# The rank-9 part of twelve chunks of a graph layer, read as nine more rows of the gathered lists

## The chip, the cores and the metric

The kernel runs on one core of one Trainium2 chip. The metric is the device time of one execution in microseconds (us); the number given is the median of several runs. The profile is one execution taken by the hardware profiler. Its engines are PE (TensorE matmuls), PEld (TensorE weight loads, which overlap PE), DVE (VectorE), ACT (ScalarE), POOL (GpSimdE) and SP (SyncE, which issues transfers). L361 means line 361 of the kernel.

## The reference, cut to what matters

There are B = 8 batches, N = 2048 nodes and D = 128 features. The matrix `adj` is 2048 x 2048, sparse: some nine entries in a row are not zero, the diagonal among them. Layer 0 and its normalisation:

```python
sj = inputs @ w_j
si = inputs @ w_i
res = si[:, :, None] + sj[:, None, :] + relation[None] * w_r + g_b
agg = jnp.einsum('bij,bjd->bid', res, inputs)
x = layernorm(x + agg @ weight + bias)
```

`res` is a sparse matrix (the relation) plus a sum of outer products. So `agg @ weight + bias` is a sparse product with y0 = x @ (weight * w_r), plus a part of low rank: node i of batch b gets si[b, i] times the sum over j of x[b, j] @ weight, plus one row that is the same for all nodes (the sj, g_b and bias terms). That is the rank-9 part: nine numbers per node (si of the eight batches, and a one) times nine rows of B x D = 1024 numbers.

Layer 1 makes two hops with `adj` itself, x1 = adj^T x and x2 = 2 adj^T x1 - x, times slices of Theta1, then bias, relu, residual and layernorm. It has no rank-9 part.

## The kernel before, in words

The nodes are cut into NC = 16 chunks of 128. A result chunk is a [128 nodes, 8 batches x 128 features] tile in two PSUM banks (`accs`).

*Opening.* Loops over the chunks load rows of `adj`, transpose them, store relation columns to DRAM (`store_rt`), make y0 (`y_chunk`, kept in `Y`) and the column sums of x, and mark which rows have entries in which block of 32 columns. `copy_r` copies `adj` columns beside the stored ones: `rr_d[c]` has, for each row n, 128 relation weights for layer 0 and 128 for layer 1. `si` holds for each chunk the eight numbers per node and a one; `make_ub` makes `ub`, the nine rows of 1024.

*Chunks 0 to 3 (ND = 4) of layer 0* are done densely (L720, all 16 row chunks). During that, the marks are turned into lists of row numbers. Each column chunk has seven: four quarter lists (rows needed by one block of 32 columns, at most eight from each row chunk, placed at that row chunk's eight places), two half lists (64 columns) and one for the whole chunk. A list has 128 places; its row numbers lie in a column of `idx`. An empty place holds PAD = 40000, past the bound of the gather, so that nothing is moved for it, and `has` is 0 there. The rows of a chunk itself are in no list: they are done as a dense diagonal block (`own_rows`, L781). `split` sets which ranks a list takes, and `lists_end` turns the found numbers into `idx` and `has`.

*Chunks 4 to 15 of layer 0* (in the order `seq`: 9 to 14, 4 to 8, 15) use the lists. For each list a gather takes rows of `rr_d` into a stage; `keep_r` (L620, L626) multiplies them by `has` and writes the columns wanted, for layer 0 into `rct` and for layer 1 into `rc`. `listed_rows` gathers the rows of y0 (from `y0_d`) into a ring of nine buffers, seven for a chunk, and multiplies them by those weights (L799): quarters, then halves, then the whole list. One round of the loop, for chunk c with the next chunk c1:

```python
            put(c)
            while jobs[0][0] == c1:
                gathers(1)
            sit = si_t(c)
            accs = acc_pair()
            own_rows(0, c, accs, True)
            rank1(c, accs, sit)
            listed_rows(0, y0_d, c, accs)
            make_u(*pending)
            z = finish0(c, accs, xr)
```

`si_t` transposes `si` on TensorE and has ScalarE copy it (L349), `rank1` does the rank-9 matmuls (L361), `make_u` takes the chunk before through transposes and a product with Theta to the store of `u`, and `finish0` adds x and normalises on VectorE and ScalarE.

*Order.* A scheduler orders each engine's instructions. `keep_in_program_order` pins an instruction behind all that was traced before it on its engine, so `keep_r(c)` comes after the layernorm of the chunk before. All gathers are chained in program order on GpSimdE, and the matmuls of `own_rows` and `listed_rows` among themselves on TensorE. The tiles of `rows4` (loads of x, `cs4`, `u`, transposed x) share five slots.

*Layer 1* makes its two hops over the same lists, from `u_d` and `y_d`, with the weights `rc`. A conditional block at the end, for matrices whose lists overflow, isn't taken here.

Of the kernel before, what the change touches and what calls it, by code (L numbers as in the profile page):

```python
# [8 lines left out]
F32 = mybir.dt.float32  # L9
# [9 lines left out]
def kernel(  # L19
# [44 lines left out]

    seq = list(range(NG4, NC - 1)) + list(range(ND, NG4)) + [NC - 1]
    PAD = 40000
    assert D == P and B == 8 and NT == 64

    y0_d = nc.dram_tensor("y0_d", (N, BD), F32).ap()
    rr_d = [  # L70
        nc.dram_tensor(f"rr_d{c}", (N, 2, P), F32).ap() for c in range(ND, NC)
    ]
    u_d = nc.dram_tensor("u_d", (N, BD), F32).ap()
    y_d = nc.dram_tensor("y_d", (N, BD), F32).ap()
# [201 lines left out]
    def store_rt():  # L276
        for c, at in stores:
            tc.keep_in_program_order(nc.sync.dma_start(
                out=rr_d[c - ND][:, 0, :].rearrange("(j p) i -> p j i", p=P), in_=at
            ))  # L280
        stores.clear()

# [62 lines left out]
    def si_t(c):  # L345
        pst = p_tr.tile([B + 1, P], F32, name=f"pst{c}", tag="pt")
        nc.tensor.transpose(pst, si[:, c, :], ident)
        sit = small.tile([B + 1, P], F32, name=f"sit{c}", tag="sit")
        nc.scalar.copy(sit, pst)  # L349
        return sit  # L350
# [7 lines left out]
    def rank1(c, accs, sit):  # L358

        for h in range(2):  # L360
            nc.tensor.matmul(  # L361
                accs[h], sit, ub[:, h * HB:(h + 1) * HB, :],
                start=False, stop=(c < ND), skip_group_check=True,
            )

    def finish0(c, accs, xr, norm=True):
# [26 lines left out]
    def copy_r(n0, n1):  # L393
        for c in seq[n0:n1]:
            tc.keep_in_program_order(
                nc.sync.dma_start(out=rr_d[c - ND][:, 1, :], in_=adj[:, c * P:(c + 1) * P])
            )

    copy_r(0, 2)


    wk = rc2[:, ND * CW:NC * CW]
    hit, two, alone = [
# [77 lines left out]
                start=False, stop=(c == NC - 2), skip_group_check=True,  # L481
            ))

    def split(rank, m, mn, lo, hi):

        nc.vector.tensor_mul(mn, m, rows_by(num, m.shape[2]))
        nc.vector.scalar_tensor_tensor(hi, rank, float(P), mn, op0=ALU.is_le, op1=ALU.mult)
        nc.vector.scalar_tensor_tensor(lo, rank, 64.0, mn, op0=ALU.is_le, op1=ALU.mult)

    def half_ranks():  # L490
        rank = p_tr.tile([P, NC, NH], F32, name="rank_h", tag="pt")
        ranks(rank, half)
        lo, hi = enc[:, :, 0:NH], enc[:, :, NH:2 * NH]
        split(rank, half, halfn, lo, hi)

        nc.vector.scalar_tensor_tensor(half, hi, 0.0, half, op0=ALU.is_equal, op1=ALU.mult)
        nc.vector.tensor_sub(hi, hi, lo)
        for t in range(2):
            nc.vector.tensor_add(both, both, pairs(half)[:, :, :, t])
# [3 lines left out]
    def chunk_ranks():  # L503
        rank = p_tr.tile([P, NC, NC], F32, name="rank_c", tag="pt")
        ranks(rank, both)
        lo, hi = enc[:, :, 2 * NH:2 * NH + NC], enc[:, :, 2 * NH + NC:96]
        split(rank, both, halfn.rearrange("p c w -> p (c w)")[:, 0:NC * NC].rearrange(
            "p (c w) -> p c w", w=NC), lo, hi)
        nc.vector.tensor_sub(hi, hi, lo)
        nc.vector.tensor_reduce(miss, both.rearrange("p c w -> p w c"), AX.X, ALU.add)  # L510

# [20 lines left out]
    def make_ub():  # L532
# [11 lines left out]
        for h in range(2):  # L544
# [3 lines left out]
                nc.tensor.matmul(pu[:, i, :], e8, b0row, start=False, stop=True)  # L548
            nc.vector.tensor_copy(ub[:, h * HB:(h + 1) * HB, :], pu)

    def lists_end(a, b, parts):

        pl = p_tr.tile([P, P], F32, name=f"pl{a}", tag="pt")
        for h, c0, src, p0, n in parts:
            tc.keep_in_program_order(nc.tensor.matmul(
                pl[64 * h:64 * h + 64, c0:c0 + n], src, ident[0:src.shape[0], p0:p0 + n],
                start=True, stop=True, skip_group_check=True, tile_position=(0, 64 * h),
            ))
        pli = pl[:, a:b]
        rown, row2 = [  # L560
            rct2[:, 5 * BD - n * P + a:5 * BD - n * P + b] for n in range(1, 3)
        ]

        nc.vector.tensor_scalar(rown, pli, 0.0, float(PAD + 1), op0=ALU.is_equal, op1=ALU.mult)
        nc.vector.scalar_tensor_tensor(rown, pli, -1.0, rown, op0=ALU.add, op1=ALU.add)
        nc.vector.tensor_copy(idx[:, a:b], rown)
        nc.vector.tensor_scalar(has[:, a:b], pli, 0.0, None, op0=ALU.is_gt)
        nc.vector.scalar_tensor_tensor(
            row2, rown, float(NC), col[:, a:b], op0=ALU.mult, op1=ALU.add
        )  # L570
        return nc.vector.tensor_copy(idr[:, a:b], row2)
# [32 lines left out]
    def gather_r(c, q, m, st, n):  # L604


        gather(
            st[:, n * m * P:(n + 1) * m * P],
            rr_d[c - ND].rearrange("n m f -> n (m f)") if m == 2 else adj128,
            idx if m == 2 else idr,  # L610
            4 * c + n if q else (LP + 2 * c, LP + 2 * c + 1, LF + c)[n], N if m == 2 else N * NC,
        )

    def keep_r(c, q, m, st):
# [54 lines left out]
    for c in range(ND):  # L669
        if c + 1 < ND:  # L670
            if NA <= c + 2 < ND:
                ar2 = load_rows(c + 2, wide[3])
            xr1 = load_x(c + 1, "xr", nc.sync)
        if c < 2:
            copy_r(2 + 5 * c, 7 + 5 * c)
        if 1 <= c <= 2:
            for n in range(8 * c - 8, 8 * c):
                tc.keep_in_program_order(
                    nc.sync.dma_start(out=y0_d[n * P:(n + 1) * P, :], in_=flat(Y[n]))
                )  # L680
        if c == 0:
            make_ub()
            rank1(0, accs, si_t(0))
        else:
            z = finish0(c, accs, xr, c > 2)
        if c + 1 < ND:
            accs1, sit = acc_pair(), si_t(c + 1)
            at2 = first_at.get(c + 2)
            for j in range(NC):
                if c == 0:  # L690
                    if j == 4:
                        tile_ranks()
                    if j == 7:
                        tile_lists()
                    if j == 10:
                        at = tile_lists_end()
                        half_ranks()
                    if j == 14:
                        chunk_ranks()
                        z = finish0(c, accs, xr, False)  # L700
                        layernorm(z, "0_0", at)
                if c == 1 and j < 2:
                    candidates(2 * j)
                    candidates(2 * j + 1)
                if c == 1 and (j > 1 and j % 2 == 0 or j == NC - 1):
                    list_round(j // 2 - (j < NC - 1))
                if c == 2:
                    if j == 4:
                        at = chunk_lists_end()
                        layernorm(z1, "0_1", at)  # L710
                    if j == 8:
                        layernorm(z, "0_2", at)
                if c > 0 or j > 11:
                    gathers(1 if j % 3 else 2, mm)
                if ar2 is not None and j % 2 == 0 and j >= 8:
                    if j == 8:
                        at2 = by_chunk(wide[0])
                    transpose_group(c + 2, ar2, at2, j // 2 - 4)
                for h in range(2):
                    mm = nc.tensor.matmul(  # L720
                        accs1[h], at1[:, j, :], Y[j][:, h * HB:(h + 1) * HB, :],
                        start=(j == 0), stop=False, skip_group_check=True,
                    )
            rank1(c + 1, accs1, sit)
            if c > 0:
                gathers(2, mm)
            at1, ar2, accs = at2, None, accs1
        if pending is not None:
            make_u(*pending)
        z1 = z  # L730
        pending, xr = (c, z, rows4(f"xt{c}")), xr1
# [54 lines left out]
    def listed_rows(i, src, c, accs):  # L786
        def rows_of(n):
            g = G[turn[2] % NG4]
            turn[2] += 1
            gather(g, src, idx, n, N)  # L790
            return g

        r = rc[:, c] if i else rct[:, c - ND]
# [12 lines left out]
    with nc.allow_non_contiguous_dma(reason="512-byte rows of a diagonal block"):  # L806
        fetch_own(0, y0_d, seq[0])
        xr = load_x(seq[0], "xs", nc.sync)
        for c, c1 in zip(seq, seq[1:] + [None]):
            if c1 is not None:  # L810
                fetch_own(0, y0_d, c1)
                xr1 = load_x(c1, "xs", nc.sync)
            put(c)
            while jobs[0][0] == c1:
                gathers(1)
            sit = si_t(c)
            accs = acc_pair()
            own_rows(0, c, accs, True)
            rank1(c, accs, sit)
            listed_rows(0, y0_d, c, accs)  # L820
            make_u(*pending)
            z = finish0(c, accs, xr)
            pending, xr = (c, z, x1t[c], held.get((1, c))), xr1
# [149 lines left out]
```

## Time and profile before

| | |
|---|---|
| time | 941.91 us, median of 3 runs (937.77 to 952.31) |
| span of the profiled execution | 945.7 us |
| busy: PE, PEld | 810.8 us (86%), 392.9 us (42%) |
| busy: DVE, ACT, POOL | 403.2 us (43%), 176.6 us (19%), 441.5 us (47%) |
| opening | 0 to 154 us |
| dense chunks and making of the lists | 154 to about 272 us |
| listed chunks of layer 0 | about 303 to 515 us |
| two hops of layer 1 | about 515 to 740 and 740 to 946 us |
| moved by transfers | 262.83 MB, 278 GB/s on the average |

The busy shares are averages over stages with different limits; what a change in one stage is worth is read from that stage. A group of the profile gives line, engine, operation, written and read tile, count, busy time and mean length, and then the idle time of the engine just before those instructions with what ended it. The chain of waits follows the work that ended last back to the start.

### The profile page before, as it was taken

How to read it: one execution, taken by the hardware profiler on the slowest of the kernel's cores; microseconds unless marked ns; L12 is line 12 of the kernel's file. 1: busy time of each engine (PE TensorE's matmuls, PEld its weight loads, DVE VectorE, ACT ScalarE, POOL GpSimd, SP SyncE). 2: the span in 40 equal slices, each digit the busy share in tenths (PEclk: the TensorE clock that was granted, in tenths of full speed). 3: DMA queues.
4: the chain of work that ended last, by engine and by line, in shares of the span. 5: the costliest groups of instructions: out<-in, count | busy, mean ns of one | idle time of the engine just before them, and what ended most of it. 6: DMA issues, size and time to landing. Idle time of an engine off the chain costs nothing.

```text
span 945.7 us, 10375 instructions
## 1 busy us (share of the span) xinstructions
PE 810.8 (86%) x3666; PEld 392.9 (42%) x3666; DVE 403.2 (43%) x627; ACT 176.6 (19%) x408; POOL 441.5 (47%) x431
## 2 busy tenths in 40 slices
PE   6999989999975878878889767889899898999992
PEld 4666653564432333423345222333333434444541
DVE  4465671539932444544345000000010045776676
ACT  3566650110111121121112000000000001111111
POOL 0000000046673676764540566767666356677750
PEclk9999998999995898987789899899999989999997
DMA  8699999962837888987775678989999689999992
GB/s 283 219 297 292 281 287 277 316 237 74 326 102 289 268 262 287 301 273 246 245 254 208 232 262 284 317 281 324 319 379 385 230 299 350 367 351 339 328 357 87
DMA packets 171183, 262.83 MB, mean 278 GB/s; under 512 B 17480, under 2 KB 122348, under 8 KB 168946
## 3 DMA queue, kind: packets, MB, share of 16 engines
q0 software_dynamic: 49280, 146.52, 44.8%
q1 hardware_dynamic: 98512, 87.83, 29.3%
q10 hardware_dynamic: 23330, 27.73, 8.3%
q8 instruction: 31, 0.51, 0.2%
q14 instruction: 30, 0.25, 0.1%
HBM read 241.63 MB, written 60.82 MB: 320 GB/s over the span
## 4 chain that ended last, share of the span: by engine, by line
PE 61%; DMA 14%; issue 11%; DVE 6%; ACT 4%; POOL 2%; another core or an unknown queue 1%; POOLq 0%; SPq 0%; ACTq 0%; DVEq 0%
PE acc L799 25%; PE acc L720 6%; DMA Y<-u_d,idx 6%; PE acc L781 5%; DMA Y<-y_d,idx 5%; PE acc L361 4%; PE acc L840 3%; PE acc L328 3%; PE acc L318 3%; PE pp L387 2%; POOL Y L592 2%; DVE rc L523 2%; PE pt_a L181 1%; ACT sq L212 1%; DMA rc<-in_adj_dram 1%
## 5 line engine op out<-in xcount | busy, mean ns | idle before, releaser
L799 PE MATMUL acc<-Y,rc 128*32 128x512 f32 (+2 forms) x896 | 245.5, 630 | 42.9 <-issue 19.1
L592 POOL DMA_INDIRECT Y<-y_d,idx x196 | 206.4, 1053 | 151.3 <-PE acc L799 91.7
L592 POOL DMA_INDIRECT stage<-rr_d,idx x84 | 94.2, 1121 | 230.4 <-PE acc L720 208.2
L592 POOL DMA_INDIRECT Y<-u_d,idx x112 | 111.3, 994 | 87.8 <-PE acc L781 30.8
L799 PEld LDWEIGHTS acc<-Y,rc 128*32 128x32 f32 (+2 forms) x896 | 63.1, 131 | 213.9 <-issue 142.3
L799 PE MATMUL acc<-Y,rct 128*32 128x512 f32 (+2 forms) x336 | 90.7, 861 | 0.0
L720 PE MATMUL acc<-Y,wide 128*128 128x512 f32 x192 | 88.2, 609 | 0.0
L361 PE MATMUL acc<-ub,sit 9*128 9x512 f32 x64 | 43.3, 807 | 36.5 <-ACT sit L349 25.8
L213 DVE TENSOR_REDUCE st<-sq 128x4 f32<-128x512 f32 x64 | 43.9, 686 | 60.5 <-ACT sq L212 31.0
L781 PE MATMUL acc<-Y,rd 128*128 128x512 f32 x140 | 67.7, 593 | 0.0
L173 DVE COPY z<-acc 128x512 f32<-128x512 f32 x9 | 6.2, 692 | 138.6 <-issue 50.4
L720 PEld LDWEIGHTS acc<-Y,wide 128*128 128x128 f32 x192 | 36.2, 195 | 41.6 <-issue 41.6
L799 PEld LDWEIGHTS acc<-Y,rct 128*32 128x32 f32 (+2 forms) x336 | 22.2, 163 | 73.3 <-issue 71.8
L212 ACT ACTIVATE sq<-z 128x512 f32<-128x512 f32 x32 | 20.1, 630 | 161.0 <-DVE z L208 105.4
L370 DVE TENSOR_TENSOR xs<-acc,xs 128x512 f32<-128x512 f32 x24 | 16.6, 692 | 78.1 <-PE acc L799 47.1
L181 PE MATMUL pt_a<-ident,rc 128*128 128x128 f32 x240 | 35.9, 286 | 7.3 <-DMA rc<-in_adj_dram 5.9
L289 DVE TENSOR_REDUCE rc<-rc 128x64 f32<-128x2048 f32 x16 | 36.5, 2282 | 13.0 <-DMA rc<-in_adj_dram 12.9
L318 PE MATMUL acc<-wx,tr_x 128*128 128x130 f32 x256 | 36.5, 286 | 3.9 <-ACT tr_x L175 3.1
L318 PEld LDWEIGHTS acc<-wx,tr_x 128*128 128x128 f32 x256 | 33.0, 195 | 14.4 <-ACT tr_x L175 6.4
L328 PE MATMUL acc<-Y,wide 128*128 128x512 f32 x64 | 36.7, 655 | 2.5 <-ACT Y L322 1.4
L361 PEld LDWEIGHTS acc<-ub,sit 9*128 9x128 f32 x64 | 13.0, 226 | 59.1 <-ACT sit L349 32.4
L181 PEld LDWEIGHTS pt_a<-ident,rc 128*128 128x128 f32 x240 | 29.4, 147 | 16.8 <-issue 14.5
(190 smaller groups left out, 935.6 us busy)
## 6 DMA issues: line engine op xcount, KB each, us to landing
rc<-in_adj_dram SPq DMA_DIRECT2D x16, 1024.0 KB
rr_d<-rct SPq DMA_DIRECT2D x12, 1024.0 KB
rr_d<-in_adj_dram SPq DMA_DIRECT2D x12, 1024.0 KB
xs<-in_x_dram SPq DMA_DIRECT2D x20, 512.0 KB
y_d<-Y SPq DMA_DIRECT2D x16, 512.0 KB
out_dram<-z ACTq DMA_DIRECT2D x16, 512.0 KB
u_d<-u ACTq DMA_DIRECT2D x14, 512.0 KB
Y<-y_d SPq DMA_DIRECT2D x14, 512.0 KB
```

What stands on the lines that cost most here:

```text
L181: nc.tensor.transpose(pt[:, i, :], s, ident)
L212: nc.scalar.activation(sq, z[:, hs, :], AF.Square)
L213: nc.vector.tensor_reduce(st[:, 2, hs], sq, AX.X, ALU.add)
L289: nc.vector.tensor_reduce(mk[:, c, :], a.rearrange("p (w f) -> p w f", f=TW), AX.X, ALU.max, apply_absolute_value=True,)
L318: nc.tensor.matmul(py[:, i, 0:D + 2], xt[b // HB][:, (b + i) % HB, :], wx, start=True, stop=True,)
L328: nc.tensor.matmul(acc0[h], first_at[0][:, c, :], Y[c][:, h * HB:(h + 1) * HB, :], start=(c == 0), stop=False, skip_group_check=True,)
L361: nc.tensor.matmul(accs[h], sit, ub[:, h * HB:(h + 1) * HB, :], start=False, stop=(c < ND), skip_group_check=True,)
L592: g = nc.gpsimd.indirect_dma_start(out=out, out_offset=None, in_=src, in_offset=bass.IndirectOffsetOnAxis(ap=ids[:, n:n + 1], axis=0), bou ...
L720: mm = nc.tensor.matmul(accs1[h], at1[:, j, :], Y[j][:, h * HB:(h + 1) * HB, :], start=(j == 0), stop=False, skip_group_check=True,)
L781: in_order(nc.tensor.matmul(accs[h], r, t[:, h * HB:(h + 1) * HB, :], start=start, stop=False, skip_group_check=True,))
L799: in_order(nc.tensor.matmul(accs[h][w * t:w * t + w], r[:, o + w * t:o + w * t + w], gs[t][:, h * HB * D:(h + 1) * HB * D], start=False, s ...
L840: in_order(nc.tensor.matmul(accs[h][:, b, :], x1t[c][:, h * HB + b, :], th[:, i, :], start=(b == 0), stop=False, skip_group_check=True,))
```

## The change

The nine numbers per node become nine more rows of weights, and the nine rows of `ub` nine more rows of y0: `y0_d` and each `rr_d[c]` get NX = N + 9 = 2057 rows. The lists then name these rows in places that no list fills. In the four quarter lists of a chunk, the eight places of its own rows are always empty: they name the eight rows of the batches. In the two half lists the last place is kept free (`most` is 127 there): it names the ninth row. The table `extra` holds what must be added to PAD in those places, and `lists_end` adds it. `more_rows`, called once before the dense chunk 0, stores the rows. Their layer 1 half is zero, and in the hops the bound of the gather stays N, so the nine rows aren't moved. The listed matmuls then do the rank-9 part of chunks 4 to 15; chunks 0 to 3 keep `rank1`. In short, with the unchanged parts left out:

```diff
-    y0_d = nc.dram_tensor("y0_d", (N, BD), F32).ap()
+    y0_d = nc.dram_tensor("y0_d", (NX, BD), F32).ap()
     rr_d = [
-        nc.dram_tensor(f"rr_d{c}", (N, 2, P), F32).ap() for c in range(ND, NC)
+        nc.dram_tensor(f"rr_d{c}", (NX, 2, P), F32).ap() for c in range(ND, NC)
...
+    extra = rct2[:, 5 * BD - 4 * P:5 * BD - 4 * P + NI]
+    nc.vector.memset(extra, 0.0)
+    xq = extra[:, 4 * ND:LP]
+    nc.vector.tensor_scalar(
+        xq, col[:, 4 * ND:LP], -8.0, num[:, 0:1], op0=ALU.mult, op1=ALU.add
+    )
...
+    nc.vector.tensor_scalar(far, extra, 0.0, None, op0=ALU.is_gt)
+    nc.vector.tensor_scalar(extra, extra, float(N - 1 - PAD), None, op0=ALU.add)
+    nc.vector.tensor_mul(extra, extra, far)
...
-        split(rank, half, halfn, lo, hi)
+        split(rank, half, halfn, lo, hi, P - 1)
...
+    def more_rows():
+
+        tc.keep_in_program_order(nc.sync.dma_start(out=y0_d[N:, :], in_=flat(ub)))
+        n = (NC - ND) * (B + 1)
+        ps = p_tr.tile([P, P], F32, name="ps", tag="pt")
+        nc.tensor.transpose(ps[0:n, :], si[:, ND:, :].rearrange("p c b -> p (c b)"), ident)
+        t = rows4("sit_all")
+        nc.vector.memset(t[:, 1, :], 0.0)
+        nc.scalar.copy(t[0:n, 0, :], ps[0:n, :])
+        for c in seq:
+            tc.keep_in_program_order(nc.sync.dma_start(
+                out=rr_d[c - ND][N:, :, :],
+                in_=t[(B + 1) * (c - ND):(B + 1) * (c - ND + 1), 0:2, :],
+            ))
...
+        nc.vector.tensor_add(rown, rown, extra[:, a:b])
         nc.vector.tensor_copy(idx[:, a:b], rown)
-        nc.vector.tensor_scalar(has[:, a:b], pli, 0.0, None, op0=ALU.is_gt)
+        nc.vector.tensor_scalar(has[:, a:b], rown, float(NX), None, op0=ALU.is_lt)
...
             make_ub()
+            more_rows()
             rank1(0, accs, si_t(0))
...
-            gather(g, src, idx, n, N)
+            gather(g, src, idx, n, src.shape[0])
...
-            sit = si_t(c)
             accs = acc_pair()
             own_rows(0, c, accs, True)
-            rank1(c, accs, sit)
             listed_rows(0, y0_d, c, accs)
```

More of the change, by code (lines that the diff above doesn't have):

```diff
@@ L66 @@
     PAD = 40000
+    NX = N + B + 1
     assert D == P and B == 8 and NT == 64
-    y0_d = nc.dram_tensor("y0_d", (N, BD), F32).ap()
+    y0_d = nc.dram_tensor("y0_d", (NX, BD), F32).ap()
     rr_d = [
-        nc.dram_tensor(f"rr_d{c}", (N, 2, P), F32).ap() for c in range(ND, NC)
+        nc.dram_tensor(f"rr_d{c}", (NX, 2, P), F32).ap() for c in range(ND, NC)
     ]
@@ L278, in store_rt @@
             tc.keep_in_program_order(nc.sync.dma_start(
-                out=rr_d[c - ND][:, 0, :].rearrange("(j p) i -> p j i", p=P), in_=at
+                out=rr_d[c - ND][0:N, 0, :].rearrange("(j p) i -> p j i", p=P), in_=at
             ))
@@ L362, in rank1 @@
                 accs[h], sit, ub[:, h * HB:(h + 1) * HB, :],
-                start=False, stop=(c < ND), skip_group_check=True,
+                start=False, stop=True, skip_group_check=True,
             )
@@ L395, in copy_r @@
             tc.keep_in_program_order(
-                nc.sync.dma_start(out=rr_d[c - ND][:, 1, :], in_=adj[:, c * P:(c + 1) * P])
+                nc.sync.dma_start(out=rr_d[c - ND][0:N, 1, :], in_=adj[:, c * P:(c + 1) * P])
             )
     copy_r(0, 2)
+    extra = rct2[:, 5 * BD - 4 * P:5 * BD - 4 * P + NI]
[4 more added lines that the diff above has]
+    )
+    far = rct2[:, 5 * BD - 3 * P:5 * BD - 3 * P + NI]
+    nc.vector.tensor_scalar(far[:, 4 * ND:LP], xq, float(B), None, op0=ALU.is_le)
+    nc.vector.tensor_mul(xq, xq, far[:, 4 * ND:LP])
+    nc.vector.tensor_scalar(far[:, 0:1], num[:, 0:1], float(P), None, op0=ALU.is_equal)
+    nc.vector.tensor_scalar(
+        extra[:, LP + 2 * ND:LF], far[:, 0:1].to_broadcast([P, NH - 2 * ND]), float(B + 1), None,
+        op0=ALU.mult,
+    )
+    nc.vector.tensor_scalar(far, extra, 0.0, None, op0=ALU.is_gt)
+    nc.vector.tensor_scalar(extra, extra, float(N - 1 - PAD), None, op0=ALU.add)
+    nc.vector.tensor_mul(extra, extra, far)
     wk = rc2[:, ND * CW:NC * CW]
@@ L482, in ranks, with split @@
             ))
-    def split(rank, m, mn, lo, hi):
+    def split(rank, m, mn, lo, hi, most):
         nc.vector.tensor_mul(mn, m, rows_by(num, m.shape[2]))
-        nc.vector.scalar_tensor_tensor(hi, rank, float(P), mn, op0=ALU.is_le, op1=ALU.mult)
+        nc.vector.scalar_tensor_tensor(hi, rank, float(most), mn, op0=ALU.is_le, op1=ALU.mult)
         nc.vector.scalar_tensor_tensor(lo, rank, 64.0, mn, op0=ALU.is_le, op1=ALU.mult)
@@ L507, in chunk_ranks @@
         split(rank, both, halfn.rearrange("p c w -> p (c w)")[:, 0:NC * NC].rearrange(
-            "p (c w) -> p c w", w=NC), lo, hi)
+            "p (c w) -> p c w", w=NC), lo, hi, P)
         nc.vector.tensor_sub(hi, hi, lo)
@@ L610, in gather_r @@
             idx if m == 2 else idr,
-            4 * c + n if q else (LP + 2 * c, LP + 2 * c + 1, LF + c)[n], N if m == 2 else N * NC,
+            4 * c + n if q else (LP + 2 * c, LP + 2 * c + 1, LF + c)[n], NX if m == 2 else N * NC,
         )
```

## The prediction

> **What bounds the kernel now.** I read the page's shares first, then its groups, then the busy time by stretch, then the chain of waits and the timeline of one chunk.
>
> ```profile
> PE 61%; DMA 14%; issue 11%; DVE 6%; ACT 4%; POOL 2%; another core or an unknown queue 1%; POOLq 0%; SPq 0%; ACTq 0%; DVEq 0%
> L361 PE MATMUL acc<-ub,sit 9*128 9x512 f32 x64 | 43.3, 807 | 36.5 <-ACT sit L349 25.8 <-issue 10.7
> L799 PE MATMUL acc<-Y,rct 128*32 128x512 f32 (+2 forms) x336 | 90.7, 861 | 0.0
> ```
>
> TensorE carries 61% of the chain. The rank-9 matmuls (L361) stand out twice: 43.3 us busy, and 36.5 us of idle TensorE just ahead of them, 25.8 of it put down to ScalarE's copy of `sit`. 48 of the 64 records, those of chunks 4 to 15, go. The next view is busy time per stretch (length, then busy us and count of PE, PEld, DVE, ACT and POOL, granted clock, DMA share, GB/s): the whole chunk loop of layer 0, then two of its periods.
>
> ```profile
> 303.00:515.00 212.00, 175.50 (x738) 74.19 (x738) 94.73 (x161) 39.17 (x81) 113.95 (x102) 0.84 0.77 256
> 339.75:356.89 17.14, 13.78 (x65) 5.87 (x69) 8.24 (x15) 3.36 (x7) 11.88 (x11) 0.90 0.81 260
> 408.48:428.92 20.44, 16.77 (x65) 6.67 (x69) 9.04 (x19) 3.36 (x7) 10.77 (x10) 0.75 0.87 287
> ```
>
> No engine is full in a period. The chain of waits shows why: the period is one serial loop (start, length, what).
>
> ```profile
> 350.47 1.54 PE acc L781 x2
> ...
> 353.87 0.63 ACT sq L212
> 354.50 0.15 ACT sit L349
> 354.65 0.04 issue
> 354.70 2.20 PE acc L361 x4
> 356.89 7.06 PE acc L799 x28
> ...
> 441.94 3.60 issue
> 445.54 3.78 PE acc L361 x4
> ```
>
> After the own-rows matmuls (L781) TensorE stands still until ScalarE, which has the two squares of the previous chunk's layernorm in its queue, has copied `sit`; then come four rank-9 records, then 28 listed ones. The listed matmuls start at 303.67, 322.60, 339.75, 356.89, 374.17, 391.30, 408.48, 428.92, 449.31, 466.54, 486.89 and 502.59: eleven periods, 198.9 us, mean 18.08. Some last 17.1 us, four about 19 to 20.4.
>
> [...] an idle of 3.60 us before 445.54 is followed by rank-9 records of 3.78 us in place of 2.20, and the long periods have a granted clock of 0.75 against 0.90. [...] The loop's periods reach 324 at a DMA share of 0.93, and two slices of the page stand at 379 and 385[...].
>
> **What the change removes.** Per chunk: a transpose (0.27 us on TensorE), the `sit` copy (0.24 on ScalarE), four rank-9 records (2.2 us, 3.8 at half clock) and the wait ahead of them (3.4 to 3.7). In a 17.1 us period TensorE's own chain is then 0.87 (pt_p) + 0.86 (L781) + 1.78 (pp) + 0.86 (L781) + 7.06 = 11.4 us. But it doesn't become 11.4, because two other loops lie just beneath. They are in the timeline of the same period (start, length, engine, line, and in brackets the idle time before).
>
> ```profile
> 343.32 0.99 POOL L592 DMA_INDIRECT Y<-y_d,idx  x1 [2.51 <-PE acc L799]
> 355.82 1.22 DVE L217 TENSOR_TENSOR xs<-xs,rs 128x1024 f32<-128x1024 f32 x1
> 355.88 2.04 POOL L592 DMA_INDIRECT Y<-y_d,idx  x1 [0.30 <-issue]
> 356.97 0.28 DVE L620 TENSOR_TENSOR rct<-stage,has 128x128 f32<-128x128 f32 x1
> 357.17 0.28 DVE L626 TENSOR_SCALAR rct<-stage,has 128x128 f32<-128x128 f32 x1
> 360.10 0.20 PEld L799 LDWEIGHTS acc<-Y,rct 128*64 128x64 f32 x4 [1.37 <-issue]
> ```
>
> *GpSimdE.* Its first gather of a period waits for a buffer that the previous chunk's quarter-list matmuls free (idle 2.51). From there ten gathers, at about 1.3 us each and two of them longer, last from 343.32 to 357.92; with 0.30 between, 14.9 us. The change leaves their number alone, so a period with ten gathers can't go below 14.9.
>
> *VectorE.* `keep_r` is pinned behind the layernorm of the previous chunk. The listed matmuls before end at 346.85, that layernorm's last operation starts at 355.82, and the half- and whole-list weights in `rct` are ready at 357.45: 10.6 us later. From the first half-list load (360.10) to the end of the chunk (363.95) are 3.85 us. 10.6 + 3.85 + about 0.1 = 14.6. Before, the weights came 2.6 us ahead of their use; now TensorE runs the quarter lists early and waits here instead. Queued behind that wait are the rest of the chunk, the transposes of the chunk before, and its `u`.
>
> So a period goes to 14.9 where ten gathers are issued and 14.6 in the last two, which have seven and five. I take 15.4 for the nine, since the transfers must fit as well: 4.5 MB a period (256 GB/s by 212 us by 1/12) plus 34 rows of 4 KB and as many of 1 KB, 0.17 MB, makes 4.7 MB; over 15.4 us that is 303 GB/s. The loop's 256 GB/s at share 0.77 scale to 332 when full, so 14.1 us: below the other two, but near enough that some gathers land late. New periods: 9 x 15.4 + 2 x 14.6 = 167.8, a saving of 31.1 us.
>
> *The first chunk.* Before, TensorE waits for chunk 3's layernorm, does four transposes (to 299.96), the rank-9 matmuls (3.71), then starts at 303.67. Without them: 3.7 us sooner.
>
> **What it adds.** Ten small VectorE operations for the table `extra`: like the 112- and 128-column ones of L156 and L162, 0.2 to 0.3 us, so 2 to 3 us; they read constants, write a region last read by the column sums of chunks 8 to 11, and are hidden, since VectorE finishes the masks at 143.5 and TensorE takes them up only at 164.4. One addition in each of two `lists_end`, 0.21 us: 0.4. In `more_rows` a transpose, a copy, a memset: under 1 us in all, and `rank1(0)` has waited for `ub` until 153.9 anyway. Thirteen stores on SyncE's queue, of 0.39 to 0.58 us like its other small issues: 5 to 7.5 us. Queued behind them are the load of rows 3, a load of x, five column copies and eight stores of Y. SyncE reaches them at 164.08, when `ub` (154.6) is long there; later it stands 43 us, until 239.40, waiting for a slot. That wait takes up the delay. The first gather, at 190.49, is paced by TensorE and needs the stores some 15 us after they were issued. Nothing is added to the hops: their bounds leave the nine rows out, as empty places were. Cost on the path, by choice: 1.5 us, between 0 and 4.
>
> Sum: 31.1 + 3.7 - 1.5 = 33.3; 941.9 - 33.3 = 908.6, say 909.
>
> **Rivals.** *The clock and the transfers take half of it back.* TensorE now idles about 3.4 us before the half lists[...]; a halved clock lengthens the rest (the listed matmuls took 8.5 us in place of 7.0), and at over 300 GB/s late gathers make the next chunk late. At a period of 16.8: 11 x (18.08 - 16.8) = 14.1, + 3.7 - 1.5 = 16.3: 926. For it speak four or five slowed periods of eleven now; against it, that idle stretch no longer stands ahead of everything else and the quarter lists don't suffer.
>
> *More than that.* With no rank-9 part, the first chunk's listed matmuls may be ordered ahead of the transposes that wait for chunk 3's layernorm. Their last gather is issued at 288.0, so they could start near 294.5, 9.2 us sooner. With 14.9 and 14.5 in the loop: 198.9 - 163.1 = 35.8; + 9.2 - 1.5 = 43.5: 898.
>
> *Slower.* `sit_all` takes one of five slots that loads, `u` and layernorm share. If that pushes the load of chunk 2's x behind the first chunk's transposes, as the next one is now (43 us, to 239.40), five copies (17.0 us) and eight stores (11.6) stand behind it: the last Y rows are stored some 28.5 us later. If then the loop gives nothing either: 941.9 + 28.5 - 3.7 + 1.5 = 968. Against it: four x slots and the `cs4` slot are free by 147.
>
> **How the numbers follow.** Forecast 0.55, more 0.15, half taken back 0.22, slower 0.08. The likeliest gives 909. Range 897 to 931: from the larger gain to a little past the half gain, leaving out the slot case, the far tail of the half gain and a start without any cost. Two per cent is 18.8 us, 923.1. Below lie the first two cases and a quarter of the third, 0.75; slower by over 2%, most of the slot case, 0.06; between, 0.19.
>
> **What would show it.** Right: L361 with 16 records, all before 303 us; listed matmuls 15 to 15.6 us apart; within them an idle of 2 to 4 us before the 128x64 weights, put down to VectorE's `rct` or a gather; GpSimdE's wait for L799 in the loop near 0.3 us; DMA share there near 0.9; the hops of the same length. Wrong: periods still at 17 us, with TensorE waiting as long for `rct` as it did for `sit`; SyncE held on a slot at 173 us; or hops that grow by what the loop lost.

## The result, and the profile after

| | before | after |
|---|---|---|
| median of 4 runs, one chip | 946.00 us (937.77 to 952.31) | 910.01 us (908.17 to 918.73) |
| ratio, 95% interval | | 0.967 (0.956 to 0.978) |
| span and granted clock of the profiled execution | 945.7 us, 0.928 | 906.4 us, 0.946 |

The prediction started from 941.91 us and forecast 33.3 us less; the medians differ by 36.0. A ratio, here and below, compares only the executions within 1.5% of the fastest of their kernel, so it isn't the quotient of the medians. The profiled executions differ by 39.3 us. The timelines of both, read at the same landmarks, say where:

| landmark (us from the start) | before | after | gained so far |
|---|---|---|---|
| chunk 3's last rank-9 matmuls end | 272.2 | 270.6 | 1.6 |
| first quarter-list weights of the first listed chunk | 303.6 | 284.9 | 18.7 |
| its whole-list weights | 309.7 | 296.3 | 13.4 |
| whole-list weights of the last listed chunk | 507.9 | 467.2 | 40.7 |
| end | 945.7 | 906.4 | 39.3 |

From the first whole list to the last, eleven periods, are 198.2 us before and 170.9 after: the loop gives 27.3, what lies ahead of it 13.4, and the hops give back 1.4.

All line numbers move on: L799 is now L837, L361 is L362, the diagonal block's L781 is L819, the transposes' L181 is L182, the layernorm's last multiplication L217 is L218, `keep_r`'s L620 and L626 are L657 and L663. First the answer for the line of the rank-9 matmuls (count, shortest, median and longest in ns, first and last start), then two groups of the page.

```profile
L362 PE MATMUL acc<-ub,sit x16: 587/588/1056, 152.2 to 270.0; 9*128 9x512 f32 x16
```

```profile
L837 PE MATMUL acc<-Y,rct 128*32 128x512 f32 (+2 forms) x336 | 93.5, 699 | 9.4 <-DMA Y<-y_d,idx 6.6
...
L182 PE MATMUL pt_p<-ident,xs 128*128 128x128 f32 x96 | 16.5, 295 | 34.2 <-DVE xs L218 25.0
```

The rank-9 records of the loop are gone and with them 36.5 us of idle TensorE ahead of them. But 34.2 us of idle now stand ahead of `pt_p`, the transposes of the chunk before, 25.0 of it put down to the layernorm. The busy time of the loop (columns as in the view of before):

```profile
284.90:484.00 199.10, 161.00 (x757) 73.84 (x758) 99.55 (x167) 42.03 (x78) 118.38 (x109) 0.89 0.89 316
```

The DMA share went from 0.77 to 0.89, the clock from 0.84 to 0.89. One of the better periods, from the timeline:

```profile
349.98 0.59 ACT L391 COPY u<-pp 128x512 f32<-128x512 f32 x1 [0.31 <-issue]
350.46 0.63 ACT L213 ACTIVATE sq<-xs 128x512 f32<-128x512 f32 x1
350.73 1.92 PE L837 MATMUL acc<-Y,rct 128*32 128x512 f32 x16
...
353.80 1.23 DVE L218 TENSOR_TENSOR xs<-xs,rs 128x1024 f32<-128x1024 f32 x1
354.94 0.29 DVE L657 TENSOR_TENSOR rct<-stage,has 128x128 f32<-128x128 f32 x1
355.14 0.28 DVE L663 TENSOR_SCALAR rct<-stage,has 128x128 f32<-128x128 f32 x1
355.17 0.41 PE L182 MATMUL pt_p<-ident,xs 128*128 128x128 f32 x2 [2.51 <-DVE xs L218]
355.50 0.20 PEld L837 LDWEIGHTS acc<-Y,rct 128*64 128x64 f32 x4 [0.17 <-DVE rct L663]
355.99 0.14 PEld L837 LDWEIGHTS acc<-Y,rct 128*64 128x64 f32 x2 [0.29 <-issue]
```

The quarter lists run at once, as forecast, and then TensorE waits 2.51 us. The scheduler has put the first two transposes of the chunk before between the quarter and the half lists. They need the layernorm (L218), so the wait goes to its name, and the weights of the half and whole lists come right behind it. The next period is the longest:

```profile
365.02 0.59 ACT L391 COPY u<-pp 128x512 f32<-128x512 f32 x1 [3.72 <-PE acc L819]
367.89 0.59 ACT L391 COPY u<-pp 128x512 f32<-128x512 f32 x1 [2.28 <-remote]
368.37 0.63 ACT L213 ACTIVATE sq<-xs 128x512 f32<-128x512 f32 x1
...
371.71 1.23 DVE L218 TENSOR_TENSOR xs<-xs,rs 128x1024 f32<-128x1024 f32 x1
373.08 0.66 PE L182 MATMUL pt_p<-ident,xs 128*128 128x128 f32 x2 [7.51 <-DVE xs L218]
373.67 0.30 PEld L837 LDWEIGHTS acc<-Y,rct 128*64 128x64 f32 x4 [0.33 <-DVE rc L657]
374.58 0.24 PEld L837 LDWEIGHTS acc<-Y,rct 128*64 128x64 f32 x2 [0.62 <-issue]
```

ScalarE's two copies of `u` come late. The first waits 3.72 us and is put down to L819, which had ended 1.3 us before, so something else let it go; the second waits 2.28 us for something the profile calls "remote" (a queue it can't name). The squares of the layernorm stand behind them in ScalarE's queue. So the layernorm ends late, TensorE idles 7.51 us, and then it runs at half clock: 0.50 is granted from 373.67 to 377.50, where the period above has 1.00 from 355.50 to 359.00, and the first half-list loads come 0.91 us apart, above 0.49 and 0.43. The eleven periods go from 13.0 to 19.9 us, mean 15.54.

### The profile page after: what moved, and what is told of

Same layout as the page of the kernel before. It is cut to its first block, busy times and chain, and to the rows that moved or that the text cites. A ratio compares the mean times of both kernels' runs of the same rounds, so it can differ in the third digit from the quotient of the medians.

```text
span 906.4 us, 10299 instructions
## 1 busy us (share of the span) xinstructions
PE 780.9 (86%) x3607; PEld 381.8 (42%) x3607; DVE 405.0 (45%) x639; ACT 175.4 (19%) x397; POOL 440.7 (49%) x431
## 3 DMA queue, kind: packets, MB, share of 16 engines
q0 software_dynamic: 49280, 148.61, 46.6%
## 5 line engine op out<-in xcount | busy, mean ns | idle before, releaser
L837 PE MATMUL acc<-Y,rc 128*32 128x512 f32 (+2 forms) x896 | 246.2, 626 | 45.7 <-DMA Y<-u_d,idx 18.7
L629 POOL DMA_INDIRECT Y<-y_d,idx x196 | 210.7, 1075 | 114.1 <-issue 46.7
L629 POOL DMA_INDIRECT stage<-rr_d,idx x84 | 89.1, 1061 | 228.7 <-PE acc L758 206.2
L837 PEld LDWEIGHTS acc<-Y,rc 128*32 128x32 f32 (+2 forms) x896 | 63.9, 130 | 216.3 <-issue 134.2
L837 PE MATMUL acc<-Y,rct 128*32 128x512 f32 (+2 forms) x336 | 93.5, 699 | 9.4 <-DMA Y<-y_d,idx 6.6
L819 PE MATMUL acc<-Y,rd 128*128 128x512 f32 x140 | 67.4, 593 | 0.0
L837 PEld LDWEIGHTS acc<-Y,rct 128*32 128x32 f32 (+2 forms) x336 | 23.5, 146 | 64.2 <-issue 51.7
L182 PE MATMUL pt_p<-ident,xs 128*128 128x128 f32 x96 | 16.5, 295 | 34.2 <-DVE xs L218 25.0
L182 PE MATMUL pt_a<-ident,rc 128*128 128x128 f32 x240 | 35.5, 284 | 6.8 <-DMA rc<-in_adj_dram 6.4
L290 DVE TENSOR_REDUCE rc<-rc 128x64 f32<-128x2048 f32 x16 | 36.5, 2280 | 6.1 <-DMA rc<-in_adj_dram 6.1
L319 PEld LDWEIGHTS acc<-wx,tr_x 128*128 128x128 f32 x256 | 32.9, 195 | 14.6 <-ACT tr_x L176 6.7
L298 DVE TENSOR_REDUCE stage<-rct 128x64 f32<-128x2048 f32 x12 | 27.4, 2286 | 21.0 <-ACT rct L176 21.0
L182 PEld LDWEIGHTS pt_a<-ident,rc 128*128 128x128 f32 x240 | 29.3, 147 | 16.2 <-issue 14.9
```

Source lines behind the costliest of these rows:

```text
L182: nc.tensor.transpose(pt[:, i, :], s, ident)
L290: nc.vector.tensor_reduce(mk[:, c, :], a.rearrange("p (w f) -> p w f", f=TW), AX.X, ALU.max, apply_absolute_value=True,)
L298: nc.vector.tensor_reduce(mkt[:, :, 4 * c:4 * c + 4], at.rearrange("p j (t f) -> p j t f", f=TW), AX.X, ALU.max, apply_absolute_value=True,)
L319: nc.tensor.matmul(py[:, i, 0:D + 2], xt[b // HB][:, (b + i) % HB, :], wx, start=True, stop=True,)
L629: g = nc.gpsimd.indirect_dma_start(out=out, out_offset=None, in_=src, in_offset=bass.IndirectOffsetOnAxis(ap=ids[:, n:n + 1], axis=0), bou ...
L819: in_order(nc.tensor.matmul(accs[h], r, t[:, h * HB:(h + 1) * HB, :], start=start, stop=False, skip_group_check=True,))
```

## Experiments

The first four kernels ran on one chip (before: 899.62 us), the next four on a second (903.40), the last four on a third (939.45). So kernels are compared by their ratio to the kernel before on the same chip, and times in the expectations by their differences. "Mean period" is the mean distance of the whole-list weight loads in the timeline.

| run | median us | ratio (95% interval) | mean period | GpSimdE's pauses, 290 to 450 us |
|---|---|---|---|---|
| e1 sit early | 875.43 | 0.978 (0.969 to 0.987) | 14.05 | 3.0 |
| e2 rank-9 late | 900.28 | 1.008 (1.006 to 1.011) | 15.95 | 19.9 |
| e3 both | 897.63 | 0.995 (0.990 to 1.000) | 17.02 | 28.5 |
| e4 weights first | 873.94 | 0.978 (0.969 to 0.987) | 14.10 | 2.6 |
| e5 the change | 877.69 | 0.972 (0.967 to 0.976) | 14.43 | 3.8 |
| e6 transposes last | 876.58 | 0.970 (0.965 to 0.975) | 14.39 | 3.0 |
| e7 own tiles for u | 874.09 | 0.968 (0.963 to 0.974) | 14.40 | 1.9 |
| e8 half rows | 871.69 | 0.967 (0.961 to 0.972) | 14.10 | 0 |
| e9 before | 930.7, one run | | 17.59 | 25.3 |
| e10 half rows, nine gathers | 904.44 | 0.966 (0.956 to 0.977) | 15.84 | 36.1 |
| e11 half rows, weights first | 906.22 | 0.967 (0.954 to 0.980) | 15.60 | 15.9 |
| e12 eleven gathers | 921.12 | 0.985 (0.974 to 0.995) | 16.13 | 15.6 |
| after, as in the result | 910.01 | 0.967 (0.956 to 0.978) | 15.54 | 17.4 |
| before, as in the result | 946.00 | | 18.02 | 35.9 |

The last column is worked out from the timeline: all time between two gathers beyond the usual 0.30 us, summed, in the traced execution. None of e1 to e8 was run on a chip as slow as that of the result.

**Was it the wait or the work?** e1 is the kernel before, with the copy of `sit` made one chunk ahead. The rank-9 matmuls stay.

```diff
+        sit = si_t(seq[0])
         for c, c1 in zip(seq, seq[1:] + [None]):
...
-            sit = si_t(c)
+            sit1 = si_t(c1) if c1 is not None else None
...
+            sit = sit1
```

> The kernel before, with the nine-row weights (sit) of a chunk made one period ahead, so that the rank-9 matmuls are all kept but no longer wait for ScalarE. Theory (after the change TensorE has idle time anyway, about 3 us ahead of the half lists, until the layernorm of the chunk before has released the weights; the rank-9 matmuls lie ahead of that idle time and fit into it): as fast as the changed kernel, 908 to 917 us, periods of the listed matmuls 15 to 16 us. Rival (wait and work each count by themselves; only the wait goes): the twelve times 2.2 us of matmuls stay on the path, 910 + 26 = about 936 us, periods near 17.5 us.

e2 is e1 with `rank1` traced and pinned behind `listed_rows`, where no idle time of TensorE follows that could take it in.

```diff
-            rank1(c, accs, sit)
             listed_rows(0, y0_d, c, accs)
+            rank1(c, accs, sit, True)
```

> As the first, but the rank-9 matmuls stand behind the listed matmuls of their chunk, at the end of the chunk's sum. They are then behind the idle time and ahead of the layernorm. Theory: the same matmuls now lengthen the loop from layernorm to layernorm, so 10 to 26 us more than the first run: 920 to 940 us, periods of 16.5 to 17.5 us. Rival (wait and work count by themselves, wherever the work stands): the same time as the first run within 0.5%.

e3 is the changed kernel with `sit = si_t(c)` and `rank1(c, accs, sit)` put back as well, so that the rank-9 part is in twice.

> The changed kernel with the transposes, copies and rank-9 matmuls of the twelve chunks put back as well, so that this part is added twice; it measures what the change adds. Theory (408 more rows in the gathers, ten small VectorE operations and 13 stores are hidden): as the kernel before, 938 to 948 us. Rival (the additions cost on the path what the first chunk and the transfers suggest, 5 us and more, hidden by the gain): 950 us and above.

e1 gains nearly what the change does: 0.978 against e5's 0.972, with overlapping intervals (the quotients of the medians are 0.973 and 0.972). The rank-9 groups, of e1 and then of e3:

```profile
L361 PE MATMUL acc<-ub,sit 9*128 9x512 f32 x64 | 33.5, 644 | 0.9 <-ACT sit L349 0.9
```

```profile
L362 PE MATMUL acc<-ub,sit 9*128 9x512 f32 x64 | 45.3, 844 | 19.3 <-ACT sit L350 19.3
```

In e1 all 64 records are there, 33.5 us, yet only 0.9 us of idle lie ahead of them where the kernel before had 36.5. Its timeline shows why the work costs nothing:

```profile
344.93 0.25 ACT L349 COPY sit<-pst 9x128 f32<-9x128 f32 x1
345.31 1.98 PE L361 MATMUL acc<-ub,sit 9*128 9x512 f32 x4
...
347.22 2.39 PE L799 MATMUL acc<-Y,rct 128*32 128x512 f32 x16
...
348.77 1.23 DVE L217 TENSOR_TENSOR xs<-xs,rs 128x1024 f32<-128x1024 f32 x1
350.05 0.44 PE L181 MATMUL pt_p<-ident,xs 128*128 128x128 f32 x2 [0.43 <-DVE xs L217]
```

The `sit` copy (of the next chunk) stands ahead of the squares now. The 1.98 us of rank-9 work run while the layernorm is under way, and TensorE waits 0.43 us for it where the changed kernel waited 2.51. In e2 the same work stands behind the lists, and the mean period is 1.9 us longer, 20.9 us over eleven; its ratio is no better than before's. e3 gives back what the change brought, by its ratio of 0.995. Its trace is of an execution of 910.4 us, with a granted clock of 0.933; others went down to 884.0 with 0.954, so its mean period of 17.02 us doesn't stand for them. The theory holds on this chip: the wait for ScalarE's `sit` was the price, and the rank-9 work is free where a wait for the layernorm follows it. The sizes: e1 brought 2.2% where 908 to 917 us would be 3 to 4%. e2 lies 24.9 us above e1, within the 10 to 26 expected, though its periods stay below the 16.5 to 17.5 expected; besides the 20.9 us in the loop, its trace has the first whole list 2.6 us later and the hops 2.0 us longer.

The price was more than the standing still, which the prediction didn't see. Two stretches, of before and of the changed kernel, hold the sixteen quarter-list matmuls of one chunk (columns as in the view of busy times above):

```profile
339.67:343.00 3.33, 3.33 (x19) 0.61 (x18) 1.17 (x5) 0.00 (x0) 1.14 (x1) 0.55 0.87 281
350.73:352.65 1.92, 1.92 (x17) 0.42 (x16) 0.83 (x2) 0.99 (x2) 1.50 (x2) 1.00 1.02 384
```

Before, the granted clock is 0.55 here, behind the wait of 3.36 us and the rank-9 matmuls. It is 0.50 to 0.59 over the quarter lists of all twelve chunks of that trace, in the short periods too, and they take 3.1 to 3.6 us, where the changed kernel needs 1.92 in nine of twelve. From the first whole list to the last, the granted clock is 0.85 before, 0.88 after and 1.00 in e1. By these two stretches, eleven periods lose about 15 us to it, an estimate; no run takes the clock and the wait apart.

**What holds the loop after that?** e4 is the changed kernel with the weights of the next chunk made on VectorE ahead of the layernorm, and `pt_p` behind the listed matmuls. e6 has only the second half of that.

```diff
             make_u(*pending)
+            while any(w[0] == c1 for w in waiting):
+                keep_r(*waiting.pop(0))
             z = finish0(c, accs, xr)
```

> The changed kernel, with VectorE's weights of the next chunk (keep_r) ordered ahead of the layernorm instead of behind it, and the transposes of the chunk before ordered behind all listed matmuls, so that no listed matmul waits for a layernorm. Theory (layernorm, GpSimdE's ten gathers of 14.9 us and the transfers at a share of 0.96 are limits of nearly the same height): little gain, 898 to 908 us, periods 14.5 to 15.2 us, the waits of TensorE now put down to gathered rows. Rival (the layernorm's loop is the one limit, TensorE's own 11.4 us the next): periods near 12 us, 870 to 880 us.

> The changed kernel, with the transposes that need the layernorm of the chunk before put behind the listed matmuls on TensorE. Theory that the trace's wait for the layernorm only names which of two waits comes last (the list weights follow the layernorm 0.2 to 0.4 us later): within 0.5% of the changed kernel. Rival, that this order costs the loop its time: 1 us and more a period less, 11 us or more below the changed kernel.

e5 is the changed kernel itself, beside e6, e7 and e8. In e7 `make_u` puts the rows of `u` in two tiles of their own.

> The changed kernel itself, beside the next three on one chip, where the kernel before takes 899.6 us. If the gain is work and waiting of TensorE alone, the ratio is again 0.967, 870 us. If transfers set what the loop can reach, it gains no more than the first experiment did (ratio 0.973 to 0.978), 875 to 880 us.

> The changed kernel, with the rows u of a chunk in two tiles of their own and stored by halves, in place of one of the five shared slots. Theory that a late slot holds ScalarE's copies of u, the squares behind them and so the layernorm: no more periods near 20 us, spread of the periods below 3 us, 5 to 12 us below the changed kernel. Rival, that the slots only pass on how late the transfers are: within 0.5%.

e8 gathers 2 KB for each row number in place of 4 (the row numbers now count half rows, so other data come, and half the bytes):

```diff
-            gather(g, src, idx, n, src.shape[0])
+            if i == 0:
+                gather(g[:, 0:HB * D], y0_d.rearrange("n (t f) -> (n t) f", t=2), idx, n, NX)
+            else:
+                gather(g, src, idx, n, src.shape[0])
```

> The changed kernel, with the list gathers of layer 0 taking only the first 2 KB of each 4 KB row, so that the products of the other half's columns are of old data; all instructions stay. Theory that the chunk loop of the changed kernel is held by transfers (share 0.89, single periods at 0.92 to 1.00): periods of 12 to 14 us, 20 to 40 us below the changed kernel. Rival, that the ten gathers' issue on GpSimdE (14.9 us) and the layernorm ahead of the list weights (14.6 us) hold it, as the prediction had it: periods of 14.6 to 15.2, within 8 us.

e5 gave 0.972 with 0.967 in its interval: it doesn't decide between its cases. e4 and e6 tried the order: neither gains over the changed kernel (e4's theory wanted 2 to 12 us, its rival 30), so the order that the trace put its waits down to isn't what costs. e7 differs from e5 by 0.4%, with overlapping intervals; but the waits it was to take away don't occur on this chip: the longest wait of a copy of `u` in e5's loop is 2.02 us. So it says nothing on the long periods of the result. e8 is 6.0 us below e5, within the rival's 8; the theory of transfers wanted 20 to 40. The busy times of e5 and then of e8, 290 to 450 us:

```profile
290.00:450.00 160.00, 136.97 (x629) 58.88 (x632) 87.63 (x147) 35.32 (x65) 118.91 (x106) 0.96 0.97 351
```

```profile
290.00:450.00 160.00, 138.20 (x646) 59.99 (x642) 90.70 (x154) 36.23 (x67) 117.61 (x106) 0.98 0.79 250
```

A DMA share of 0.97 at 351 GB/s looks like a bound. It isn't what sets the period: with 250 GB/s at 0.79 the same 106 gathers are issued in the same time. GpSimdE's column tells why. In e8, 117.6 us in gathers and 106 times 0.30 between them are 149.4 of 160 us, and its timeline has no pause at all between the first and the last gather there. A short period of e8:

```profile
327.56 2.40 PE L840 MATMUL acc<-Y,rct 128*32 128x512 f32 x16
...
330.63 1.22 DVE L218 TENSOR_TENSOR xs<-xs,rs 128x1024 f32<-128x1024 f32 x1
331.97 0.28 DVE L663 TENSOR_SCALAR rct<-stage,has 128x128 f32<-128x128 f32 x1
332.00 0.41 PE L182 MATMUL pt_p<-ident,xs 128*128 128x128 f32 x2 [2.04 <-DVE xs L218]
```

Three periods of this trace last 12.91 or 12.92 us, two more 13.0 to 13.1: I read this as the loop through the layernorm and the list weights when nothing disturbs it. Ten gathers at 1.11 and 0.30 are 14.1, the mean period. So on this chip GpSimdE's issue holds the loop, with transfers and layernorm close under it. The same pauses, 0 to 3.8 us, are in e1 and e4 to e7: each of them has come to that limit, whatever was done about the rest.

**One gather less, one more.** These were to test that, with e11 for the layernorm (half rows together with the order of e4). e10 is half rows with the fourth quarter list using the rows of the third; e12 the changed kernel with an eleventh gather, of 128 bytes a row into a tile that nobody reads. They came to the third chip, with e9, the kernel before, for its trace.

```diff
+            if i == 0 and n == LP + 2 * c:
+                t = small.tile([P, 32], F32, name=f"more{c}", tag="more", bufs=1)
+                gather(t, y0_d.rearrange("n (t f) -> (n t) f", t=32), idx, n, NX)
```

> The kernel before, for its trace on the chip of the experiments, where it takes 900 us in place of 942. Theory: its undisturbed period, 17.15 us, is a chain of TensorE, ScalarE and VectorE and the same on any chip; what is lost beyond it on the chip of the result (mean 18.02) is the halved clock after idle time. So a mean period of 17.1 to 17.3 here, and its whole-list loads of the first and last chunk 188 to 190 us apart. Rival, that the loop is as slow as there: 197 us and more.

> The kernel with half rows, less one gather in each chunk of layer 0: the fourth quarter list takes the rows of the third, so the products with these rows are of other rows. Theory that with half rows the loop is GpSimdE's alone (106 gathers without a pause, 1.11 us and 0.30 between, 1.41 each): 1.2 to 1.4 us a period less, a mean of 12.7 to 12.95, 12 to 16 us below the kernel with half rows. Rival, that TensorE, ScalarE and VectorE hold it there: within 4 us of it.

> Half rows, and the list weights of the next chunk made on VectorE ahead of the layernorm, with the transposes behind the listed matmuls. Theory that GpSimdE holds the loop: a mean period of 13.9 to 14.2 as with half rows alone, within 4 us of it. Rival, that the layernorm ahead of the list weights holds it, as the prediction had it at 14.6: a mean of 12 to 13, 12 us or more below half rows alone.

> The changed kernel with one more gather in each chunk of layer 0, of 128 bytes for each row and read by nobody, so that GpSimdE has eleven to issue where it had ten. Theory that GpSimdE's issue holds the loop of the changed kernel, or comes so close to it that it counts: 1.0 to 1.4 us a period more, 11 to 17 us above the changed kernel. Rival, that the transfers hold it and GpSimdE has time to spare: within 4 us of it.

On this chip the loop is held otherwise. e9: six periods near 17.0 as expected, but one of 18.0, three of 18.3 to 20.4 and a last one of 15.1; the mean is 17.59, and the eleven take 193.5 us, between the 188 to 190 expected and the rival's 197. e10 and e11 have ratios like e8's, but e8 didn't run here. Measured against the changed kernel of the result, which this chip resembles (939 and 946 us before), they gain nothing: e10's GpSimdE pauses 36.1 us in 160, so the missing gather can't show. Each has a wait like this one, of e10 and then of e11:

```profile
305.06 1.29 DVE L371 TENSOR_TENSOR xs<-acc,xs 128x512 f32<-128x512 f32 x2 [16.32 <-remote]
```

```profile
340.26 0.69 DVE L374 TENSOR_TENSOR xs<-acc,xs 128x512 f32<-128x512 f32 x1 [11.22 <-remote]
```

The addition of x waits 16 and 11 us for a releaser without a name, most likely x's own load; then everything behind the layernorm is late. Between such waits e11 has four periods of 11.2 to 11.3 where e10 has 12.9: the order of e4 does shorten the layernorm's loop, by 1.6 us, but the mean is set elsewhere. e12 is 1.3 to 1.9% above the changed kernel, 12 to 17 us of 940, as the theory had it, but for another reason in the main: in the trace the first whole list comes 12.5 us later than in the result's, and the loop is only 6.5 us longer, where 11 to 15 were expected. I don't count it for GpSimdE. So that limit rests on the unbroken gathers and on e8 alone; taking a gather away on a chip of the first kind wasn't tried.

## Why the prediction was right, and where it was not

*The total* was 909, measured 910.01. That it came so near is partly luck: two of its terms missed in opposite directions (the loop by 3.8 us, the first chunk by 9.7), and before itself was measured 4 us higher than the prediction's start.

*The rank-9 wait*: right, and shown by e1 to e3. The removed work (2.2 us a chunk) was rightly left out of the saving: it lay beside the layernorm's wait. But the 7.06 us that the prediction took for TensorE's own listed work hold the quarter lists at about half clock (0.56 granted from 356.89 to 360.10). In the changed kernel's period at 350.73 the same work is 1.92 + 3.85, or 5.8 us. The sum wasn't touched by it, since it came from the two limits beneath.

*The loop*: 31.1 forecast, 27.3 in the traces: a mean period of 15.54 for a forecast one of 15.25 (167.8 by 11). The nearness is partly chance. The two limits beneath were both taken from one period and were too long: ten gathers are 14.9 in the prediction, but 1.09 us each in the changed kernel's trace with 0.30 between, 13.9; the layernorm's loop was 14.6 and is 12.92 undisturbed. The difference, 1.6, lies between the second addition (L370) and the first square: 5.6 us in the period that the prediction read, 4.0 in e8's. In the first, the two copies of `u` ahead of the squares waited 2.19 and 0.89 us, in e8 1.36 and 0.31. The `sit` transpose isn't the reason: e3 has it too, and 4.0. Why the copies waited less isn't shown. Over these lower limits lie the late periods, up to 19.9, that the prediction had as "some gathers land late". In the longest period it was the copies of `u` that came late, for a reason that stays open; GpSimdE paused 17.4 us in 160 of this loop. On the faster chips, without these waits, the change reaches 14.43, below the floor of 14.9 that I had given it.

*The first chunk*: 3.7 forecast, 13.4 in the traces. The term was mis-sized, but how much of it belongs to the change is open. In e9, the kernel before again, the first whole list is at 301.6, 8.1 us earlier than in the trace of before; in e1 and e3, which keep the rank-9 part, at 299.5 and 299.6, against 299.1 in e5. In three of the slower traces a copy of `u` holds up chunk 3's layernorm: it waits 10.37 us in the trace of before, 7.17 after, 4.91 in e9. The rival "more" was right that the listed matmuls would be ordered ahead of chunk 3's transposes. What ends TensorE's long wait there, before and then after:

```profile
298.88 1.09 PE L181 MATMUL pt_p<-ident,xr 128*128 128x128 f32 x4 [10.55 <-DVE xr L217]
284.89 4.47 PE L837 MATMUL acc<-Y,rct 128*32 128x512 f32 x6 [6.06 <-DMA Y<-y_d,idx]
```

Before, TensorE stands 10.55 us for the layernorm; after, the quarter lists run meanwhile and wait only for their own rows. They start 18.7 us sooner, where the rival said 9.2, and the whole list 13.4, since the rows of the quarter lists land one list after the other and the transposes still come in between. The change does take this wait out, but how long it would have been is a matter of the late copy.

*The additions*: 1.5 chosen between 0 and 4; chunk 3 ends 1.6 us earlier than before, so nothing of them shows. The queue of the gathers moved 146.52 MB before and 148.61 after: the 2.09 MB more are the loop's 408 rows of 4 KB and of 1 KB, so for empty places, and for the nine rows in the hops, nothing is moved. The slot for `sit_all` did no harm; the rival "slower" had no start.

*What was to show it.* Right: L362 with 16 records, idle of 2 to 4 us ahead of the 128x64 weights in the better periods, DMA share near 0.9, hops of nearly the same length (439.2 us from the last whole list to the end, 437.8 before).

Wrong: periods scatter from 13.0 to 19.9 where 15 to 15.6 was said, the idle is put down to the layernorm by way of `pt_p`, not to `rct`, and GpSimdE still waits up to 5.2 us for L837.

*The clock.* The rival "half taken back" is right in kind: some waits ahead of the half lists had a halved clock behind them (0.50 granted and 0.91 us between loads behind 373.08, 1.00 and 0.49 behind 355.17). In the trace after, the length of a wait doesn't decide: of two waits of 2.51 us the one before 355.17 left the granted clock at 1.00, while behind the one before 463.52 it was 0.50, to 465.87; a wait of 3.08 us before 403.44 left it at 1.00. What decides isn't shown, and no run separates what these halvings cost.

## What to carry to other kernels

A small product that a serial loop waits for (here 9 x 128 numbers, copied by an engine whose queue holds longer work) is best made one round ahead: that edit alone, of four lines, brought nearly all that the moved computation did, on the chips where both could be compared with before. When a wait is taken out, the next limits come from counts over the whole stage (gathers by mean issue and gap, bytes by a measured rate such as e5's 351 GB/s, the undisturbed loop of waits), not from one period; and a transfer share of 0.97 is no proof of a bound until halving the bytes has been tried.

## What the runs showed of the hardware

A gather's issue takes GpSimdE about 1.0 us and 0.30 to the next, for 4 KB a row as for 128 bytes (in e12 0.99 and a median of 1.005); some (4 to 18% between 290 and 450 us) take 1.3 to 2.05, so the mean of that stretch is 1.03 to 1.15, by trace.

The core moved 351 to 359 GB/s over 160 us (e5, e1) at a DMA share of 0.97 to 0.99. One slice of 22.7 us of the page after stands at 391, so these means are no cap.

One kernel differs by 4 to 5% between chips: before took 900 and 903 us on two, 939 and 946 in the other runs. The changed kernel's last whole list to its end took 419.7 us in e5 and 439.2 in the result. Waits for "remote" releasers stand in all traces of the slower chips and in none of e1 to e8. The profiles of e1 to e8 also give the gathers' time to landing (a median of 8.4 us in e5's loop, 4.3 in e8's) and the others don't, so part of it may be naming; whether loads land later on those chips is open.
